# Offsets of a deformable convolution as a thread of their own in a four-layer network kernel

## The chip, the cores and the metric

The kernel runs on one core of a Trainium2 chip. The core has a matmul engine (TensorE, PE in the profile; PEld are its weight loads), VectorE (DVE), ScalarE (ACT), GpSimd (POOL) and SyncE (SP), which issues most of the transfers. Each engine works through its own instructions in program order, and waits between engines go over semaphores. The metric is the device time of one execution in microseconds (us). The times of the kernel before are 12860.76, 12851.66 and 12822.62 us, median 12851.66 us.

## The reference

The input is a batch of four images of 56x56 positions with 128 channels, in float32. Four residual layers follow each other; each takes the group norm of x (32 groups) and adds its result to x. Layers 0 and 3 are window attention, then attention over all 3136 positions with four heads, then an MLP of 128 to 512 to 128. Layer 1 is a selective scan in four directions after a depthwise 3x3 convolution. Layer 2, which the change is about, is a deformable 3x3 convolution:

```python
x = x + _L0_conv_ref(_gn(x), ...)
x = x + _L1_conv_ref(_gn(x), ...)
x = x + _L2_conv_ref(_gn(x), L2_conv_kernel, L2_conv_bias, L2_conv_offset_w, L2_conv_offset_b)
x = x + _L3_conv_ref(_gn(x), ...)
...
offsets = lax.conv_general_dilated(x, offset_w, ...) + offset_b
dy, dx = (offsets[..., 0], offsets[..., 1])
py = jnp.arange(H, ...)[None, :, None, None] + ky + dy
px = jnp.arange(W, ...)[None, None, :, None] + kx + dx
y0 = jnp.floor(py)
x0 = jnp.floor(px)
...
val = gather(y0i, x0i) * ((1 - wy) * (1 - wx))[..., None] + ...
out = jnp.einsum('bhwkc,kcf->bhwf', val, kernel.reshape(KK, C, F))
```

For each position and each of the nine taps a small convolution says how far from the regular place the sample is taken. Four neighbours are fetched, weighted and summed, and the nine samples are multiplied by the kernel.

## The kernel before

Channels lie on the 128 partitions and an image is a row of 3136 columns, cut into seven chunks of 448 (`NCK`, `CH`). Two images are held at a time (`x_of(b)` takes the buffer by the image's parity), so the layers of neighbouring images are staggered. `run` (L1476) sets the order. For image b it emits the attention of layer 0; then, woven together, the MLP of layer 0 and the convolution stage of layer 1 for image b (`first_half`, L1464) with layer 2 of image b-1 (`deform`, L1282); then the scan of layer 1 (`mamba`, L763); and then layer 3 of image b-1 (`last_layer`, L1471). Image 3 has no successor, so its layer 2 goes beside the MLP of layer 3 of image 2, and the last call is layer 3 of image 3 with nothing beside it.

`weave` (L650) takes two generators, a main and a side one. Each yields a number, a planned duration, and the one whose sum is lower is continued (the side one if equal). So the numbers set only the order in which the instructions of the two stand in each engine's queue.

`deform` has two parts. The first, L1310 to L1391, finds the offsets: it takes the group norm, writes the normed image x to a table in device memory with positions as rows (transposes at L1324, copies at L1325, eight DMAs on the SP queue at L1333), runs the offset convolution as 63 matmuls of 32 output rows in two groups (L1353), adds the bias (L1362), transposes (L1365), and then works out indices `idx` and weights `wts` in twelve VectorE steps per group (L1372 to L1390). Its yields sum up to 7 x 0.6 + 8 x 0.8 = 10.6. The second part, L1392 to L1456, has 84 units (chunk, row of three taps, block of 112 positions). A unit is three indirect DMAs on the POOL queue (`gather`, L1300), three VectorE operations (`weigh`, L1406 to L1408), six transposing matmuls and a ScalarE copy (`turn`, L1418 and L1419), and, four units later, a product with the kernel (L1426). `lead = 4` units are gathered ahead into six buffers; the first four are asked for in the middle of the first part (L1382), as soon as the first group's indices stand. A unit yields 1.9. The weights of both parts, 973 KB, are one pack "L2" that `deform` loads at its head.

`mlp` (L662) is a pipeline over the seven chunks. What matters here is that its PSUM banks depend on whether it is alone: `bufs={"mm": 6 if alone else 2, "pc": 2 if alone else 1}` (L667). All matmul results but the centred rows ("pc") go through the "mm" banks. `last_layer` passes `side is None` for `alone`. The yields of an MLP sum up to 69.8, those of the convolution stage of layer 1 (`mamba_conv`, L772) to 91.0.

Of the kernel before, what the change touches and what calls it, by code (L numbers as in the profile page):

```python
# [10 lines left out]
F32 = mybir.dt.float32  # L11
F32R = mybir.dt.float32r
I32 = mybir.dt.int32
# [6 lines left out]
P = 128  # L20
# [34 lines left out]
def _swin_cols():  # L55
# [7 lines left out]
    "L0": _swin_cols(),  # L63
    "L1": [("w_in", 512), ("w_xproj", 2 * NX), ("w_out", 256), ("conv_w", 18), ("conv_b", 2), ("b_dt", 2),
           ("A_log", 2 * NST), ("D", 2), ("ln_w", 2), ("ln_b", 2), ("w_dt", 256)],
    "L2": [("kernel", KK * 128), ("offset_w", KK * 32), ("bias", 1), ("offset_b", 1), ("base", 2 * KK * NTB)],
    "L3": _swin_cols(),
}

# [9 lines left out]
class _Net:  # L79
# [1199 lines left out]
                )  # L1279
                nc.sync.dma_start(t[TR * TR :], z[:1])  # L1280

    def deform(self, b):  # L1282

# [3 lines left out]
        tab = self.tables[b]  # L1287
        n2 = NTB * KK
        nq = CH // QB
        lead = 4  # L1290
        units = [(c, j, i) for c in range(NCK) for j in range(KK // 3) for i in range(nq)]
        with tc.tile_pool(name="df", bufs=1, side="right") as s1, tc.tile_pool(name="df_ps", bufs=1, space=PSUM, side="right") as s1x:
            self.load("L2", s1, nc.sync)
            w = self.w["L2"]
            idx = s1.tile([QB, n2], I32, tag="idx", name="idx")
            wts = s1.tile([QB, n2, 4], F32, tag="wts", name="wts")
            wps = s1x.tile([P, 3, nq * KK, 4], F32, tag="wt", name="wt")
            patch = {}

# [7 lines left out]
                        in_offset=bass.IndirectOffsetOnAxis(ap=idx[:, n : n + 1], axis=0),  # L1307
                    )

            with tc.tile_pool(name="dc", bufs=1, side="right") as sb, tc.tile_pool(name="dc_ps", bufs=4, space=PSUM, side="right") as ps:  # L1310
                bank = lambda name: ps.tile([P, 512], F32, tag="mm", name=name)
                gp = sb.tile([P, TR, TR], F32, tag="gp", name="gp")
                nc.gpsimd.memset(gp, 0.0)
                gn = self.group_norm(b, sb, bank)
                xg = sb.tile([P, L], F32, tag="xg", name="xgd")
                gt = sb.tile([QB, NTB, P], F32, tag="gt", name="gt")
                tv = tab[: TR * TR].rearrange("(t r x) (k c) -> r x t k c", r=2, x=TR, k=2)
                for c in range(NCK):
                    cols = slice(c * CH, (c + 1) * CH)
                    self.gn_apply(xg[:, cols], x[:, cols], gn)  # L1320
                    pt = bank("pgt")
                    for i in range(nq):
                        t = c * nq + i
                        nc.tensor.transpose(pt[:QB, i * P : (i + 1) * P], xg[:, t * QB : (t + 1) * QB], self.ident)  # L1324
                    nc.scalar.copy(gt[:, c * nq : (c + 1) * nq, :].rearrange("q t c -> q (t c)"), pt[:QB, :])  # L1325
                    if c in (3, NCK - 1):
                        ts = slice(0 if c == 3 else 4 * nq, (c + 1) * nq)
                        for k in range(2):
                            for r in range(2):

                                y = r + 1 - k
                                dst = tv[y % 2, 1 : 1 + HW, y // 2 + ts.start : y // 2 + ts.stop, k, :]
                                nc.sync.dma_start(dst, gt[r * HW : (r + 1) * HW, ts, :])  # L1333
                    yield 0.6
                gv = xg.rearrange("p (h w) -> p h w", w=HW)
                of = sb.tile([P, 2, CH], F32, tag="of", name="of")
                pos, fl, up = (sb.tile([QB, 2 * n2], F32, tag=n, name=n) for n in ("pos", "fl", "up"))
                fi = sb.tile([QB, 2 * n2], I32, tag="fi", name="fi")
                ix = sb.tile([QB, n2], F32, tag="ix", name="ix")
                fr = sb.tile([QB, 2, 2 * n2], F32, tag="fr", name="fr")  # L1340
                for g in range(2):
                    n = min(4, NCK - 4 * g)
                    rows = slice(32 * g, min(HW, 32 * g + 32))
                    nc.vector.tensor_copy(gp[:, 1 + rows.start : 1 + rows.stop, 1 : 1 + HW], gv[:, rows, :])
                base = w["base"][:QB, :]
                for g in range(2):
                    n = min(4, NCK - 4 * g)
                    pf = bank("pf")
                    for k in range(KK):
                        ky, kx = k // 3, k % 3  # L1350
                        for j in range(n):
                            c = 4 * g + j
                            nc.tensor.matmul(  # L1353
                                pf[32 * j : 32 * j + 32, :CH].rearrange("p (h w) -> p h w", w=HW),
                                lhsT=w["offset_w"][:, k * 32 : (k + 1) * 32],
                                rhs=gp[:, 8 * c + ky : 8 * c + ky + 8, kx : kx + HW],
                                start=(k == 0),
                                stop=(k == KK - 1),
                            )
                        if k % 3 == 2:  # L1360
                            yield 0.8
                    nc.scalar.activation(of[: 32 * n, g, :], pf[: 32 * n, :CH], AF.Identity, bias=w["offset_b"][: 32 * n, :])  # L1362
                    pt = bank("pof")
                    for i in range(nq):
                        nc.tensor.transpose(pt[:QB, i * P : i * P + 32 * n], of[: 32 * n, g, i * QB : (i + 1) * QB], self.ident[: 32 * n, : 32 * n])  # L1365
                    src = pt[:QB, :].rearrange("q (i j s) -> q j i s", j=4, s=32)[:, :n, :, : 2 * KK]

                    ts = slice(4 * g * nq, (4 * g + n) * nq)
                    ns = slice(ts.start * KK, ts.stop * KK)
                    both = lambda t: t[:, 2 * ns.start : 2 * ns.stop]  # L1370
                    view = lambda t: both(t).rearrange("q (j i s) -> q j i s", j=n, s=2 * KK)
                    nc.vector.tensor_add(view(pos), src, view(base))  # L1372

                    nc.vector.tensor_scalar(both(pos), both(pos), -1.0, float(HW), ALU.max, ALU.min)
                    nc.vector.tensor_copy(both(fi), both(pos))
                    nc.vector.tensor_copy(both(fl), both(fi))
                    nc.vector.tensor_tensor(both(up), both(fl), both(pos), ALU.is_gt)
                    nc.vector.tensor_sub(both(fl), both(fl), both(up))
                    fl2 = both(fl).rearrange("q (n s) -> q n s", s=2)
                    nc.vector.scalar_tensor_tensor(ix[:, ns], fl2[:, :, 0], float(TR), fl2[:, :, 1], ALU.mult, ALU.add)  # L1380
                    nc.vector.tensor_scalar_add(idx[:, ns], ix[:, ns], float(TR + 1))
                    if g == 0:  # L1382
                        for u in range(lead):
                            gather(u)
                    nc.vector.tensor_sub(both(fr[:, 1, :]), both(pos), both(fl))
                    nc.vector.tensor_scalar(both(fr[:, 0, :]), both(fr[:, 1, :]), -1.0, 1.0, ALU.mult, ALU.add)
                    for k in range(4):
                        wy = fr[:, k % 2, :].rearrange("q (n s) -> q n s", s=2)[:, :, 0]
                        wx = fr[:, k // 2, :].rearrange("q (n s) -> q n s", s=2)[:, :, 1]
                        nc.vector.tensor_mul(wts[:, ns, k], wy[:, ns], wx[:, ns])  # L1390
                    yield 0.8  # L1391
# [81 lines left out]
            x1, oT = self.swin_attention("L3", b, s1)  # L1473
            self.weave(self.mlp("L3", b, x1, oT, True, side is None), side)

    def run(self):  # L1476
        self.nc.sync.dma_start(self.xs[0], self.x_in[0])
        self.swin_prepare("L0")
        self.swin_prepare("L3")
        self.mamba_prepare()  # L1480
        self.deform_prepare()
        self.nc.sync.dma_start(self.xs[1], self.x_in[1])
        for b in range(self.B):
            for c in range(NCK):
                self.stats(b, c)
            with ExitStack() as mb:
                s1, made = ExitStack(), {}
                made["at"] = self.swin_attention("L0", b, s1)
                self.weave(self.first_half(b, s1, mb, made, b == 0), self.deform(b - 1) if b > 0 else None)
                self.mamba(b, made["pool"], made)  # L1490
            if b > 0:
                self.last_layer(b - 1, self.deform(b) if b == self.B - 1 else None)
        self.last_layer(self.B - 1)


# [53 lines left out]
def _packs(inputs):  # L1549
    def getter(layer):  # L1550
        return lambda n: np.ascontiguousarray(inputs[f"{layer}_conv_{n}"])

    parts = {"C": _constants(), "L0": _swin_pack(getter("L0")), "L1": _mamba_pack(getter("L1")),
             "L2": _deform_pack(getter("L2")), "L3": _swin_pack(getter("L3"))}
# [29 lines left out]
```

## Time and profile before

| what | us |
|---|---|
| median of the runs | 12851.66 |
| the profiled execution's own time | 12830.39 |
| its span | 12828.6 |
| layer 0 MLP and convolution of image 0, nothing beside them | 878 to 1073 |
| the same for image 1, beside layer 2 of image 0 | 2932 to 3399 |
| the same for image 2, beside layer 2 of image 1 | 6096 to 6562 |
| the same for image 3, beside layer 2 of image 2 | 9251 to 9720 |
| layer 3 MLP of images 0 and 1, nothing beside it | 5261 to 5329, 8419 to 8487 |
| layer 3 MLP of image 2, beside layer 2 of image 3 | 11579 to 12000 |

The stretches are cut where one kind of instruction ends and the next begins, so that each holds one stage. Over the span PE is busy for 11489.0 us (90%), DVE 9912.4 (77%), POOL 9659.9 (75%) and ACT 7461.7 (58%). The rest of the span is attention (PE busy all the time) and scan (DVE and POOL busy all the time), which the change does not touch. In a row of the view by stretches each engine has its busy time and, in brackets, its number of instructions. In a row of the view in order of time stand start, duration, engine, line, operation, output and inputs, shape and count, and in square brackets how long the engine had been idle and what ended that.

### The profile page before, as it was taken

What the parts mean: (1) busy time and instruction counts of PE and PEld (TensorE: products, weight loads), DVE (VectorE), ACT (ScalarE), POOL (GpSimd) and SP (SyncE); (2) the same over time, 40 slices, a digit from 0 to 9 for tenths busy, and PEclk for the clock granted to TensorE, in tenths of its full rate; (3) what the DMA queues carried; (4) which work ended last, traced back from release to release, by engine and by line L of the source; (5) the groups of instructions that cost most, each with busy time, mean ns of one, the idle gap of its engine ahead of it and who ended that gap; (6) DMA issues with size and microseconds to landing.
All of it is one profiled execution on the core that took longest, in us unless ns stands there. A gap on an engine that the chain in (4) does not pass through costs nothing.

```text
span 12828.6 us, 220823 instructions
## 1 busy us (share of the span) xinstructions
PE 11489.0 (90%) x86708; PEld 7481.4 (58%) x86708; DVE 9912.4 (77%) x12555; ACT 7461.7 (58%) x19090; POOL 9659.9 (75%) x6636
## 2 busy tenths in 40 slices
PE   5998998997799899999789989989978998996699
PEld 3546886543588755454368875545436886543454
DVE  4758997776999867576799977747589997776675
ACT  3567776553577655656367765565536776553356
POOL 1866996686799748578689975848778996686487
PEclk8999999998899999999889999999989999997899
DMA  1000000004200000000420000000051000004200
GB/s 62 1 1 17 5 5 2 1 1 123 86 5 5 3 1 1 11 1 1 144 66 5 5 2 1 1 11 1 19 155 38 5 5 1 1 1 138 62 1 6
DMA packets 155231, 321.13 MB, mean 25 GB/s; under 512 B 19612, under 2 KB 88400, under 8 KB 153936
## 3 DMA queue, kind: packets, MB, share of 16 engines
q0 software_dynamic: 80640, 231.28, 6.2%
q1 hardware_dynamic: 73264, 74.14, 1.9%
q8 instruction: 685, 11.22, 0.4%
q14 instruction: 354, 2.90, 0.1%
q10 hardware_dynamic: 288, 1.59, 0.0%
HBM read 259.03 MB, written 47.90 MB: 24 GB/s over the span
## 4 chain that ended last, share of the span: by engine, by line
PE 63%; DVE 20%; ACT 7%; issue 4%; POOL 4%; another core or an unknown queue 2%; SPq 1%; DMA 0%; DVEq 0%; ACTq 0%; POOLq 0%
PE pm L367 17%; DVE hs L1115 12%; PE po L573 10%; PE pst L546 5%; PE yt L1133 4%; PE dbu L1097 4%; PE pst L537 3%; POOL hs L1124 3%; PE pyb L1149 3%; PE pd L562 2%; DVE dgb L1001 2%; PE pss L276 1%; PE ph L703 1%; PE pt L1068 1%
## 5 line engine op out<-in xcount | busy, mean ns | idle before, releaser
L368 DVE TENSOR_REDUCE mx<-pm 128x1 f32<-128x256 f32 (+2 forms) x5600 | 3263.0, 618 | 1082.1 <-PE pm L367 1065.3
L557 POOL TENSOR_TENSOR es<-es,e 128x896 f32<-128x896 f32 x1824 | 3769.4, 2090 | 297.3 <-ACT e L547 249.5
L547 ACT ACTIVATE e<-pst 128x448 f32<-128x448 f32 (+1 forms) x5600 | 2591.8, 549 | 1857.9 <-PE pst L546 999.4
L1115 DVE TENSOR_TENSOR_SCAN hs<-da,dbu 128x928 f32<-128x928 f32 x1792 | 3631.8, 2069 | 50.2 <-ACT dbu L1108 27.6
L1124 POOL TENSOR_TENSOR hs<-hs,cb 128x896 f32<-128x896 f32 x1792 | 3460.3, 1941 | 22.4 <-ACT carry L1119 17.3
L367 PE MATMUL pm<-ks,qs 32*128 32x256 f32 (+2 forms) x11200 | 3133.0, 586 | 13.9 <-DVE nm L389 7.8
L546 PE MATMUL pst<-qs,ks 32*128 32x448 f32 x11200 | 2285.8, 536 | 0.0
L1133 PE MATMUL yt<-w_C,hs 128*116 128x128 f32 x14336 | 1863.6, 273 | 1.2 <-POOL hs L1124 1.2
L367 PEld LDWEIGHTS pm<-ks,qs 32*128 32x128 f32 x11200 | 1217.3, 186 | 975.3 <-DVE mx L368 598.1
L537 PE MATMUL pst<-nm,sel 32*128 32x448 f32 x5600 | 1659.9, 552 | 0.0
L1133 PEld LDWEIGHTS yt<-w_C,hs 128*116 128x116 f32 x14336 | 1569.1, 135 | 2.1 <-POOL hs L1124 2.1
L1097 PE MATMUL dbu<-dgb,ut 112*128 112x224 f32 x7168 | 1254.7, 297 | 271.3 <-DVE hs L1115 271.3
L546 PEld LDWEIGHTS pst<-qs,ks 32*128 32x128 f32 x11200 | 1369.8, 185 | 53.0
L1305 POOL DMA_INDIRECT g<-tab,idx x1008 | 1050.7, 1042 | 447.2 <-issue 264.7
L573 PE MATMUL po<-e,va 128*32 128x448 f32 (+1 forms) x11200 | 1350.9, 551 | 0.0
L1097 PEld LDWEIGHTS dbu<-dgb,ut 112*128 112x128 f32 x7168 | 942.0, 191 | 536.4 <-DVE hs L1115 526.6
L1051 ACT ACTIVATE da<-dl,A 128x112 f32<-128x112 f32 x3584 | 1193.9, 382 | 0.1
L294 POOL TENSOR_TENSOR pz<-s,m 64x784 f32<-64x784 f32 x128 | 191.8, 1499 | 847.6 <-DVE m L291 615.3
L537 PEld LDWEIGHTS pst<-nm,sel 32*128 32x128 f32 x5600 | 689.8, 184 | 180.2 <-issue 152.2
L573 PEld LDWEIGHTS po<-e,va 128*32 128x32 f32 (+1 forms) x11200 | 222.2, 107 | 966.7 <-issue 894.7
L1119 ACT COPY carry<-hs 128x32 f32<-128x32 f32 x1792 | 396.5, 221 | 624.0 <-DVE hs L1115 616.1
L557 POOL TENSOR_TENSOR es<-e 128x896 f32<-128x896 f32 x112 | 231.7, 2092 | 588.2 <-ACT e L547 588.2
(233 smaller groups left out, 15885.4 us busy)
## 6 DMA issues: line engine op xcount, KB each, us to landing
g<-tab,idx POOLq DMA_INDIRECT x1008
tab<-zero SPq DMA_DIRECT2D x4, 3364.0 KB
dl_d<-dl SPq DMA_DIRECT2D x28, 448.0 KB
dl<-dl_d SPq DMA_DIRECT2D x56, 224.0 KB
tab<-gt SPq DMA_DIRECT2D x16, 448.0 KB
out_dram<-x SPq DMA_DIRECT2D x28, 224.0 KB
tab<-gt SPq DMA_DIRECT2D x16, 336.0 KB
w_L<-in_L_dram SPq DMA_DIRECT2D x4, 973.0 KB
```

What stands on the lines that cost most here:

```text
L367: nc.tensor.matmul(pm[:, :m], lhsT=qs[head(h), q.start : q.start + P], rhs=ks[head(h), keys], start=True, stop=True)
L368: nc.vector.tensor_reduce(mx[:, home[i][1], h, kc : kc + 1], pm[:, :m], AX.X, ALU.max)
L537: nc.tensor.matmul(pst[g, h][:, :CH], lhsT=self.sel[head(h), :], rhs=nm[head(h), part(g // NKB)], start=True, stop=False)
L546: nc.tensor.matmul(t[:, :CH], lhsT=ks[head(h), k * KB : (k + 1) * KB], rhs=qs[head(h), part(qc)], start=False, stop=True)
L547: nc.scalar.activation(es[g, p][:nk, j, :], t[:nk, :CH], AF.Exp, scale=SCALE)
L557: nc.gpsimd.tensor_tensor(s, es[g - 1, p][:nk] if k == 1 else s, es[g, p][:nk], ALU.add)
L573: nc.tensor.matmul(m["po"][head(h), :CH], lhsT=va[:nk, k, head(h)], rhs=src(h)[:nk], start=(k == 0), stop=(k == NKB - 1))
L1051: nc.scalar.activation(m["da"][:, :, n, 2:], dl(), AF.Exp, scale=A[:, j, n : n + 1])
L1097: nc.tensor.matmul(pu[:, 8 * h : 8 * h + 8, 2 + tb * TB : 2 + (tb + 1) * TB], lhsT=made[g]["ut", 2 * r + tb][:, d, :], rhs=made["r", g // ...
L1115: nc.vector.tensor_tensor_scan(flat(pairs[u // 2][:, d % 2]), flat(made[g]["da"][:, r]), flat(banks.pop(u)), 0.0, ALU.mult, ALU.add)
L1124: nc.gpsimd.tensor_tensor(hs, hs, made["r", g // 2]["cb"][:, :, r * HW : (r + 1) * HW], ALU.mult)
L1133: nc.tensor.matmul(sums[q][:YR, e * P : (e + 1) * P], lhsT=hs[:, n, :], rhs=self.ident, start=(n == 0), stop=(n == NST // 2 - 1), is_trans ...
```

## The change

The first part of `deform` becomes a generator of its own, `offsets(b, where, pace)`, with all its yields multiplied by `pace`. Its results `idx` and `wts` live in a pool "dx" of their own, which stays open until the units of that image are done. The pack "L2" is split: "O2" with what the offsets need, and "L2" with kernel and bias. `deform` keeps the units alone; it asks for the first four gathers at its head. `run` places the offsets of image 0 after the scan of image 0, with nothing beside them; those of images 1 and 2 beside the MLP of layer 3 of the preceding image, with pace 4; those of image 3 directly before its `deform`, in one thread with it, as before.

```diff
-    "L2": [("kernel", KK * 128), ("offset_w", KK * 32), ("bias", 1), ("offset_b", 1), ("base", 2 * KK * NTB)],
+    "L2": [("kernel", KK * 128), ("bias", 1)],
+    "O2": [("offset_w", KK * 32), ("offset_b", 1), ("base", 2 * KK * NTB)],
...
+    def offsets(self, b, where, pace=1):
...
+        s1 = where.enter_context(tc.tile_pool(name="dx", bufs=1, side="right"))
+        idx = s1.tile([QB, n2], I32, tag="idx", name="idx")
+        wts = s1.tile([QB, n2, 4], F32, tag="wts", name="wts")
+        self.found = idx, wts
+        with tc.tile_pool(name="dc", bufs=1, side="right") as sb, tc.tile_pool(name="dc_ps", bufs=4, space=PSUM, side="right") as ps:
+            bank = lambda name: ps.tile([P, 512], F32, tag="mm", name=name)
+            self.load("O2", sb, nc.sync)
+            w = self.w["O2"]
...
+                yield 0.6 * pace
...
+                    if k % 3 == 2:
+                        yield 0.8 * pace
...
+                    nc.vector.tensor_mul(wts[:, ns, k], wy[:, ns], wx[:, ns])
+                yield 0.8 * pace
+
+    def deform(self, b):
...
+        idx, wts = self.found
         lead = 4
...
             self.load("L2", s1, nc.sync)
             w = self.w["L2"]
-            idx = s1.tile([QB, n2], I32, tag="idx", name="idx")
-            wts = s1.tile([QB, n2, 4], F32, tag="wts", name="wts")
...
-                    if g == 0:
-                        for u in range(lead):
-                            gather(u)
...
+            for u in range(lead):
+                gather(u)
...
+    def both(self, *threads):
+        for t in threads:
+            yield from t
...
                 self.weave(self.first_half(b, s1, mb, made, b == 0), self.deform(b - 1) if b > 0 else None)
+                if b > 0:
+                    where.close()
                 self.mamba(b, made["pool"], made)
-            if b > 0:
-                self.last_layer(b - 1, self.deform(b) if b == self.B - 1 else None)
+            where = ExitStack()
+            if b == 0:
+                self.weave(self.offsets(b, where))
+            elif b + 1 < self.B:
+                self.last_layer(b - 1, self.offsets(b, where, 4))
+            else:
+                self.last_layer(b - 1, self.both(self.offsets(b, where), self.deform(b)))
+                where.close()
         self.last_layer(self.B - 1)
```

More of the change, by code (lines that the diff above doesn't have):

```diff
@@ L1280, in deform_prepare @@
                 nc.sync.dma_start(t[TR * TR :], z[:1])
-    def deform(self, b):
+    def offsets(self, b, where, pace=1):
         nc, tc, x = self.nc, self.tc, self.x_of(b)
@@ L1289, in deform @@
         nq = CH // QB
+        s1 = where.enter_context(tc.tile_pool(name="dx", bufs=1, side="right"))
[6 more added lines that the diff above has]
+            w = self.w["O2"]
+            gp = sb.tile([P, TR, TR], F32, tag="gp", name="gp")
+            nc.gpsimd.memset(gp, 0.0)
+            gn = self.group_norm(b, sb, bank)
+            xg = sb.tile([P, L], F32, tag="xg", name="xgd")
+            gt = sb.tile([QB, NTB, P], F32, tag="gt", name="gt")
+            tv = tab[: TR * TR].rearrange("(t r x) (k c) -> r x t k c", r=2, x=TR, k=2)
+            for c in range(NCK):
+                cols = slice(c * CH, (c + 1) * CH)
+                self.gn_apply(xg[:, cols], x[:, cols], gn)
+                pt = bank("pgt")
+                for i in range(nq):
+                    t = c * nq + i
+                    nc.tensor.transpose(pt[:QB, i * P : (i + 1) * P], xg[:, t * QB : (t + 1) * QB], self.ident)
+                nc.scalar.copy(gt[:, c * nq : (c + 1) * nq, :].rearrange("q t c -> q (t c)"), pt[:QB, :])
+                if c in (3, NCK - 1):
+                    ts = slice(0 if c == 3 else 4 * nq, (c + 1) * nq)
+                    for k in range(2):
+                        for r in range(2):
+                            y = r + 1 - k
+                            dst = tv[y % 2, 1 : 1 + HW, y // 2 + ts.start : y // 2 + ts.stop, k, :]
+                            nc.sync.dma_start(dst, gt[r * HW : (r + 1) * HW, ts, :])
+                yield 0.6 * pace
+            gv = xg.rearrange("p (h w) -> p h w", w=HW)
+            of = sb.tile([P, 2, CH], F32, tag="of", name="of")
+            pos, fl, up = (sb.tile([QB, 2 * n2], F32, tag=n, name=n) for n in ("pos", "fl", "up"))
+            fi = sb.tile([QB, 2 * n2], I32, tag="fi", name="fi")
+            ix = sb.tile([QB, n2], F32, tag="ix", name="ix")
+            fr = sb.tile([QB, 2, 2 * n2], F32, tag="fr", name="fr")
+            for g in range(2):
+                n = min(4, NCK - 4 * g)
+                rows = slice(32 * g, min(HW, 32 * g + 32))
+                nc.vector.tensor_copy(gp[:, 1 + rows.start : 1 + rows.stop, 1 : 1 + HW], gv[:, rows, :])
+            base = w["base"][:QB, :]
+            for g in range(2):
+                n = min(4, NCK - 4 * g)
+                pf = bank("pf")
+                for k in range(KK):
+                    ky, kx = k // 3, k % 3
+                    for j in range(n):
+                        c = 4 * g + j
+                        nc.tensor.matmul(
+                            pf[32 * j : 32 * j + 32, :CH].rearrange("p (h w) -> p h w", w=HW),
+                            lhsT=w["offset_w"][:, k * 32 : (k + 1) * 32],
+                            rhs=gp[:, 8 * c + ky : 8 * c + ky + 8, kx : kx + HW],
+                            start=(k == 0),
+                            stop=(k == KK - 1),
+                        )
+                    if k % 3 == 2:
+                        yield 0.8 * pace
+                nc.scalar.activation(of[: 32 * n, g, :], pf[: 32 * n, :CH], AF.Identity, bias=w["offset_b"][: 32 * n, :])
+                pt = bank("pof")
+                for i in range(nq):
+                    nc.tensor.transpose(pt[:QB, i * P : i * P + 32 * n], of[: 32 * n, g, i * QB : (i + 1) * QB], self.ident[: 32 * n, : 32 * n])
+                src = pt[:QB, :].rearrange("q (i j s) -> q j i s", j=4, s=32)[:, :n, :, : 2 * KK]
+                ts = slice(4 * g * nq, (4 * g + n) * nq)
+                ns = slice(ts.start * KK, ts.stop * KK)
+                both = lambda t: t[:, 2 * ns.start : 2 * ns.stop]
+                view = lambda t: both(t).rearrange("q (j i s) -> q j i s", j=n, s=2 * KK)
+                nc.vector.tensor_add(view(pos), src, view(base))
+                nc.vector.tensor_scalar(both(pos), both(pos), -1.0, float(HW), ALU.max, ALU.min)
+                nc.vector.tensor_copy(both(fi), both(pos))
+                nc.vector.tensor_copy(both(fl), both(fi))
+                nc.vector.tensor_tensor(both(up), both(fl), both(pos), ALU.is_gt)
+                nc.vector.tensor_sub(both(fl), both(fl), both(up))
+                fl2 = both(fl).rearrange("q (n s) -> q n s", s=2)
+                nc.vector.scalar_tensor_tensor(ix[:, ns], fl2[:, :, 0], float(TR), fl2[:, :, 1], ALU.mult, ALU.add)
+                nc.vector.tensor_scalar_add(idx[:, ns], ix[:, ns], float(TR + 1))
+                nc.vector.tensor_sub(both(fr[:, 1, :]), both(pos), both(fl))
+                nc.vector.tensor_scalar(both(fr[:, 0, :]), both(fr[:, 1, :]), -1.0, 1.0, ALU.mult, ALU.add)
+                for k in range(4):
+                    wy = fr[:, k % 2, :].rearrange("q (n s) -> q n s", s=2)[:, :, 0]
+                    wx = fr[:, k // 2, :].rearrange("q (n s) -> q n s", s=2)[:, :, 1]
+                    nc.vector.tensor_mul(wts[:, ns, k], wy[:, ns], wx[:, ns])
+                yield 0.8 * pace
@@ L1290, in deform @@
+    def deform(self, b):
+        nc, tc, x = self.nc, self.tc, self.x_of(b)
+        tab = self.tables[b]
+        nq = CH // QB
+        idx, wts = self.found
         lead = 4
@@ L1308, in gather @@
                     )
[L1310 to L1381, printed above, removed]
-                    if g == 0:
-                        for u in range(lead):
-                            gather(u)
[L1385 to L1391, printed above, removed]
@@ L1553, in _packs @@
     parts = {"C": _constants(), "L0": _swin_pack(getter("L0")), "L1": _mamba_pack(getter("L1")),
-             "L2": _deform_pack(getter("L2")), "L3": _swin_pack(getter("L3"))}
+             "L2": _deform_pack(getter("L2")), "O2": _deform_pack(getter("L2")), "L3": _swin_pack(getter("L3"))}
     out = {}
```

## The prediction

> **What bounds it now.** I read the view by stretches first, because the change moves work between stages with different limits. Columns: stretch, its length, busy time (instructions) of PE, PEld, DVE, ACT and POOL, granted clock, DMA share, GB/s.
>
> ```profile
> 2932.00:3399.00 467.00, 339.06 (x1225) 174.94 (x1224) 379.43 (x480) 168.89 (x288) 291.30 (x276) 0.81 0.49 142
> 5261.00:5329.00 68.00, 62.04 (x166) 29.64 (x162) 40.10 (x40) 46.05 (x62) 17.73 (x18) 0.97 0.13 41
> 11579.00:12000.00 421.00, 242.08 (x966) 132.68 (x962) 293.32 (x346) 89.72 (x164) 251.00 (x267) 0.74 0.52 152
> ```
>
> In the first stretch (image 1's MLP and convolution with image 0's layer 2; two more are like it) DVE is the fullest engine, at 81%. The second, the MLP of layer 3 alone, is PE's, at 91%. The third is layer 2 of image 3 beside an MLP; its end is that of layer 2.
>
> The order of time at the head of the first stretch shows what the offsets cost there.
>
> ```profile
> 2939.49 0.35 DVE L134 BATCH_NORM_AGGREGATE gn_mv<-gn_st 128x2 f32<-128x42 f32 x1 [1.30 <-POOL oTi L599]
> ...
> 2943.70 0.51 DVE L150 TENSOR_SCALAR xgd<-x,gn_mean,gn_rstd 128x448 f32<-128x448 f32 x1
> ...
> 2959.31 5.83 PE L1353 MATMUL pf<-gp,w_L 128*32 128x448 f32 x48
> ...
> 2973.43 1.13 POOL L1305 DMA_INDIRECT g<-tab,idx  x1 [6.12 <-DVE idx L1381]
> ...
> 2985.83 0.96 DVE L1390 TENSOR_TENSOR wts<-fr 112x108 f32<-112x108 f32 x4
> 2986.63 1.02 DVE L1406 TENSOR_TENSOR pa<-g,wt 112x768 f32<-112x768 f32 x1
> ```
>
> Attention's last write frees the memory at 2939.5; the first unit is weighed at 2986.6, behind the last weights. For 47.1 us there are no units, though they set the stage's end: the last is weighed until 3376.2, the last statistics end at 3383.2, while the convolution's last DVE work ends at 3364.9.
>
> The same view in the MLP alone:
>
> ```profile
> 5283.79 2.95 DVE L688 RECIPROCAL ln_sq<-ln_sq 128x448 f32<-128x448 f32 x1 [1.83 <-ACT ln_sq L187]
> 5284.84 1.67 PE L703 MATMUL ph<-xn,w_L 128*128 128x448 f32 x4
> 5286.34 0.92 PE L160 MATMUL ln_pc<-x,w_C 128*128 128x448 f32 x2
> 5286.66 0.58 DVE L715 SCALAR_TENSOR_TENSOR x<-py,w_L,x 128x448 f32<-128x448 f32 x1
> 5287.16 0.61 DVE L692 TENSOR_TENSOR ln_sq<-ln_pc,ln_sq 128x448 f32<-128x448 f32 x1
> ...
> 5293.11 1.29 PE L703 MATMUL ph<-xn,w_L 128*128 128x448 f32 x3
> ```
>
> A chunk takes 8.27 us (5284.84 to 5293.11) with eleven matmuls of 0.75 us back to back: PE has no slack here, so what PE gets in addition lengthens the stage. Note too that the centred rows' matmul (L160) starts at 5286.34, before DVE has read the rows before them (L692, 5287.16), and that L715, which empties a bank, stands behind the reciprocal.
>
> **Step 1, units without the offsets before them (three stages).** `deform` can gather as soon as memory is free. Its first weighing follows two further gathers of 1.24 us and the landing; in image 3's units, where DVE waits for the DMA, 3.5 us pass from the start of a unit's third gather to the weighing (11934.47 to 11937.95). So 2939.5 + 0.3 + 2.5 + 3.5 = 2945.8 instead of 2986.6. What the MLP did in those 47 us must now be done beside units. Counting L1408, 32 units were done at the MLP's last store (3131.1; 4.5 us a unit) and 80 at the convolution's end (3363.8; 4.85 a unit). By the yields the MLP (69.8) now spans 69.8 / 1.9 = 36.7 units, and the convolution (91.0) the remaining 47.3: 36.7 x 4.5 + 47.3 x 4.85 = 394.5, so the last weighing ends at 3340.3, plus the same 7.0 us of tail, 3347.3 instead of 3383.2. **-35.9 a stage; I take -35, three times: -105.** Fifteen gathers now stand at the head of POOL's queue, before the MLP's addition (L683); only L715, many us later, needs that. The smaller load of "L2" on SP is wanted by the first product, some 20 us in; the load of 973 KB had landed within 20 us at 2959.3. Ends: -25 (a dense start: the first seven units took 5.4 us each) and -42 (the MLP costs nothing beside units; in image 3's tail without it a unit still takes 4.2).
>
> **Step 2, image 0's offsets with nothing beside them.** They come after the scan of image 0, and every engine's queue holds them ahead of the next attention. Added up from the rows above and those between: group norm 4.2 (2939.49 to 2943.70), seven applications 3.6, the first padded copy (L1344) 1.0, first group of matmuls 5.83 + 2.46 = 8.3, bias and transposes 1.4, second group 2.46 + 4.71 = 7.2, bias and transposes 1.4, twelve DVE steps 4.5: 31.6, and about 1.4 for the hand-overs. **+33** (30 to 40). The fill of `gp` (2.9 on POOL), the load of "O2" and the eight table DMAs (12.0 of SP's issuing) lie beside it; uncovered, the load could add some 5.
>
> **Step 3, images 1 and 2's offsets beside an MLP (two stages).** Both are PE work now.
> - Head: PE's queue begins with the group norm, which waits for the freed memory. The MLP's first matmul, at 5263.17 today, stands behind 5267.4 + 5.7 = 5273.1; its start-up had gaps, so I count +8.5.
> - Matmuls: transposes 3.5, offset convolution 15.5, two turns 1.2 and two waits of 0.75 for the bias on ACT: +21.5.
> - Banks: with "mm" at 2 the second hidden matmul waits until L715 has emptied the result's bank, which waits for the reciprocal (5286.74); with one "pc" bank L160 waits for L692 (5287.77). Followed through one chunk, the period comes to 10.15 instead of 8.27. Over seven chunks +13; offset matmuls lie in these holes in the first four chunks and the last two have no reciprocal, so +8.
> - DVE: gn, copies and 2 x 12 steps, 15 us on an engine busy 40 of 68. Mostly hidden, but a lump of 4.5 delays the reciprocal twice: +3. Some of the early transposes lie in start-up gaps: -3.
>
> Sum +38; **twice, +76**. Ends: +25 (only PE's 21.5 and part of the head) and +50 (with pace 1 beside image 3, the first hidden matmul came at 11618.9, 39.8 after the freed memory, against 7.4 in the MLP alone, so 32 there, and 13 for banks and some more at the end). The table DMAs stand on SP ahead of the stores and the loads of the next image; they are issued within the first quarter, and the last load is what the next stage waits for (8.5 us of DVE's idle time at L123, as before).
>
> Here the Trainium skill speaks against the change: "Perfetto Trace Analysis", sections "Matmuls" and "Matmul Optimizations", wants independent matmul groups to rotate through different PSUM banks and all eight used. Taken as a price, with nothing filling the holes, the rows give 13 a stage and the sum below rises by 10; I take 8, because here the side thread's matmuls fill most holes.
>
> **Step 4, image 3.** Its gathers were asked for inside the first part (11613.2 by the order of time); now they come behind the last weights, at 11633, because the unit's buffers lie where the offsets' were. First weighing at 11639.2 instead of 11632.6: **+7** (0 to 20; 20 if the gathers, not the weighing, set the pace of the stage. Units wait for landings only in the second half).
>
> **Sum:** -105 + 33 + 76 + 7 = **+11 us**. The profiled execution took 12830.4 (span 12828.6), so 12841 on its scale; it lies 21 us below the median shown, on whose scale I forecast 12851.7 + 11 = **12863**. A measurement of this kernel can tell about 0.3%, 38.6 us, from no change; the runs shown spread over 38. So the forecast is: no change that can be told.
>
> **Rivals.**
> - *The MLPs take the offsets badly (slower).* One place, layer 3 of images 0 and 1: two banks keep PE waiting in every chunk, and the offsets' chain, in order on PE, adds its whole length: 13 + 42 = +55 each. -105 + 33 + 110 + 7 = +45: 12897. For it: PE is full there, and the 32 us at image 3. Against it: pace 4 spreads the chain over 42.4 of 69.8. It decides from +52 a stage.
> - *The three stages are DVE's (slower).* Then only the DVE work taken out counts: about 16 us of 379 at 81%, 20 a stage. -60 + 33 + 76 + 7 = +56: 12908. For it: DVE is at 98% beside the convolution. Against it: beside the MLP it is near 80%, and in the first 40 us about half idle.
> - *Both ends good (faster).* The MLP is nearly free beside units (-42), and the layer-3 MLPs hide the chain in PE's own waits (+22): -126 + 33 + 44 + 7 = -42: 12810. For it: 4.5 us a unit with the MLP, 4.2 without. Against it: PE is full.
>
> That the move does not take place in time can be left out: nothing in queue order keeps the gathers behind the next attention's end.
>
> **How the numbers follow.** Forecast 0.45, first rival 0.20, second 0.17, faster 0.18. The ends together: 3 x -25 + 40 + 100 + 20 = +85 and 3 x -42 + 30 + 50 + 0 = -46; the range is 12800 to 12935. From the cases: faster 0.18, same 0.44, slower 0.38; the forecast's own spread crosses the upper bound a little.
>
> **What would show it.** First weighing about 6 us after attention's end in three stages, and these near 431 us instead of 467 (between 425 and 442 is right). A hole of about 33 us without scan or attention after image 0's scan. Layer 3's MLP of images 0 and 1 near 106 us, with PE waiting at L703 on L715 and at L160 on L692. Image 3's stage longer by 7. I am wrong if an MLP stage grows by over 50 or under 25, if units in the three stages take over 5 us each, or if something in attention slows, which now runs with the indices' 5 KB per partition kept.

## The result, and the profile after

The kernel with the change takes 12904.12 us (median of 6 runs, 12894.7 to 12916.09), the kernel before, on the same chip, 12852.24 us (6 runs, 12822.62 to 12867.71). The ratio is 1.0043, with a 95% interval of 1.003 to 1.0056: slower by 52 us, a little more than the 0.3% that can be told from no change. The profiled execution is the slowest of the six, 12916.09 us with a span of 12914.3, so the two traces differ by 85.7 us where the medians differ by 51.9. The stages show where.

The view by stretches of the kernel after has the same columns as before. The rows are image 1's MLP and convolution with image 0's layer 2; layer 3's MLP of image 0, now with the offsets of image 1; layer 2 of image 3; and image 0's offsets with nothing beside them, up to the end of the group norm of the attention behind them.

```profile
2998.60:3428.50 429.90, 306.21 (x1038) 162.66 (x1038) 358.83 (x431) 162.69 (x274) 282.00 (x274) 0.82 0.51 146
5294.80:5412.00 117.20, 92.43 (x320) 39.09 (x320) 50.98 (x76) 51.21 (x71) 19.72 (x18) 0.89 0.20 55
11663.70:12084.40 420.70, 240.88 (x950) 132.91 (x950) 287.44 (x335) 88.02 (x162) 246.34 (x262) 0.74 0.54 152
2197.20:2229.50 32.30, 21.54 (x170) 11.10 (x170) 16.26 (x49) 5.80 (x12) 2.78 (x4) 0.87 0.40 100
```

The first stage is shorter, as meant, and its DVE is fuller: 358.83 of 429.90 is 83%. The second row carries the loss. PE worked 92.43 of 117.20 us, 79%, where the MLP alone had it at 91%. So the stage has grown by more than the work put into it: PE waits there. Its granted clock is lower too, 0.89 where the MLP alone had 0.97. That is a mean of full and half clock. Here are two of the five stretches at half clock, two matmuls in the first of them, and two at full clock (each matmul leaves two records):

```profile
5310.00:5316.90 6.90, 5.58 (x10) 2.53 (x10) 2.08 (x4) 2.14 (x4) 1.13 (x1) 0.51 0.00 0
5320.30:5323.70 3.40, 3.15 (x8) 1.93 (x9) 1.57 (x4) 1.99 (x3) 0.00 (x0) 0.50 0.14 33
...
5311.81 1.70 PE L161 MATMUL ln_pc<-x,w_C 128*128 128x448 f32 x2
5313.31 1.70 PE L677 MATMUL py<-oTi,w_L 128*128 128x448 f32 x2
...
5325.26 1.67 PE L704 MATMUL ph<-xn,w_L 128*128 128x448 f32 x4
```

From one matmul's start to the next it is 1.50 us in the first stretch, where the MLP alone had 0.75, and the two matmuls that start in the second (5321.44, shown below) take 2.79 us instead of 1.67. The five stretches hold 25.6 us, 20.1 of them with PE busy; in the MLP alone there was one stretch of 3.4, all of it busy. As a matmul takes half as long at full clock, some 8 us of the 55 that the stage has grown by are slower matmuls (half of 20.1 - 3.4; an estimate).

The table measures every stage in the same way in both traces, from attention's last write on POOL (from the scan's end for image 0) to what follows the stage. The 3.3 us of image 0 before are the group norm of the attention behind it.

| part | forecast | before, us | after, us | difference |
|---|---|---|---|---|
| the three stages, up to the first scan | -105 | 459.4, 459.9, 462.3 | 429.9, 430.7, 430.7 | -90.3 |
| image 0's offsets alone, with the attention behind them | +33 | 3.3 + 764.8 | 32.3 + 769.1 | +33.3 |
| layer 3 MLP of images 0 and 1, up to the last store | +76 | 62.1, 62.1 | 117.2, 117.7 | +110.7 |
| layer 2 of image 3 | +7 | 411.0 | 420.7 | +9.7 |
| sum | +11 | | | +63.4 |

The remaining 22.3 us of the two spans' difference lie ahead of the change. From the start to the end of image 0's first attention the execution took 885.0 us before and 908.1 after; in the profiles of the experiments, which share that code, it took 877.8 to 888.9. I take it for variation of that one execution. The 63.4 us of the touched stages are of the size of the medians' 51.9.

The order of time of the kernel after shows both ends of the first of the three stages.

```profile
2997.49 1.13 POOL L600 TENSOR_TENSOR oTi<-ou,rest 128x448 f32<-128x448 f32 x1 [5.89 <-DVE rest L596]
2998.91 1.13 POOL L1398 DMA_INDIRECT g<-tab,idx  x1 [0.29 <-POOL oTi L600]
...
3005.40 0.96 DVE L1419 TENSOR_TENSOR pa<-g,wt 112x768 f32<-112x768 f32 x1 [8.06 <-DMA g<-tab,idx]
...
3395.41 0.95 DVE L1421 TENSOR_TENSOR g<-g,pa 112x768 f32<-112x768 f32 x1
...
3407.80 1.09 DVE L872 SCALAR_TENSOR_TENSOR dl<-dl,sp_u 128x896 f32<-128x896 f32 x1
...
3408.81 0.68 DVE L1443 SCALAR_TENSOR_TENSOR x<-pdo,w_L,x 128x448 f32<-128x448 f32 x1
...
3412.03 0.27 DVE L938 MEMSET carry<- 128x256 f32 x1 [1.88 <-DMA dl_d<-dl]
```

The first gather leaves POOL 0.3 us after attention's last write, and the first weighing comes 6.8 us after it instead of 47. The units end 397.7 us after it (436.7 before). But the last addition to x (L1443) now stands in DVE's queue right behind the convolution's last step (L872), 13.1 us after the last unit's work, where the tail was 6.3. And ahead of the scan DVE waits until the convolution's `dl` is written (L938). The units no longer set the end of the stage alone.

The same view at the head of the MLP of layer 3:

```profile
5294.83 0.34 DVE L135 BATCH_NORM_AGGREGATE gn_mv<-gn_st 128x2 f32<-128x42 f32 x1 [1.30 <-POOL oTi L600]
...
5299.60 1.10 PE L1311 MATMUL pgt<-w_C,xgd 128*112 128x128 f32 x4 [2.44 <-DVE xgd L151]
...
5307.58 2.95 DVE L689 RECIPROCAL ln_sq<-ln_sq 128x448 f32<-128x448 f32 x1 [0.73 <-ACT ln_sq L188]
5310.45 0.41 DVE L151 TENSOR_SCALAR xgd<-x,gn_mean,gn_rstd 128x448 f32<-128x448 f32 x1
...
5310.92 1.10 PE L1311 MATMUL pgt<-w_C,xgd 128*112 128x128 f32 x4 [4.04 <-DVE xgd L151]
...
5317.20 2.95 DVE L689 RECIPROCAL ln_sq<-ln_sq 128x448 f32<-128x448 f32 x1 [1.48 <-ACT ln_sq L188]
5320.07 0.41 DVE L151 TENSOR_SCALAR xgd<-x,gn_mean,gn_rstd 128x448 f32<-128x448 f32 x1
...
5320.55 1.10 PE L1311 MATMUL pgt<-w_C,xgd 128*112 128x128 f32 x4 [4.04 <-DVE xgd L151]
5321.44 2.79 PE L704 MATMUL ph<-xn,w_L 128*128 128x448 f32 x4
```

The offsets' application of the group norm (L151) takes 0.41 us, but it stands in DVE's queue behind a reciprocal of the MLP (L689) of 2.95 us. The transposes (L1311) need it, and they stand in PE's queue ahead of the MLP's matmuls. So PE waits 4.04 us for a step of 0.41, twice in these lines, and the first hidden matmul (L704) comes at 5321.4, 26.6 us after attention's last write; before it came after 7.4.

The view of waits of this stage (engine, tile and line that waits, what for; us in total, times, longest):

```profile
PE pgt L1311 <- DVE xgd L151: 14.4, 5, 4.0
...
PEld ln_pc L161 <- DVE ln_sq L693: 5.9, 2, 4.4
PEld ph L704 <- ACT h L705: 5.5, 6, 1.4
...
PE gn_pm L137 <- DVE gn_mv L135: 5.5, 1, 5.5
```

The first row is that queue order: 14.4 us in five pieces. The next two are banks: a new matmul's weight load waits until the bank's reader is done; the matmuls themselves wait there for 4.5 and 2.2 us. The last is the group norm at the head of PE's queue; all but 0.5 us of that wait lies ahead of the stage's start. Late in the stage, where the offsets are over and the clock is full, the banks stand alone in the order of time:

```profile
5386.74 0.92 PE L704 MATMUL ph<-xn,w_L 128*128 128x448 f32 x2
5388.38 1.02 PE L704 MATMUL ph<-xn,w_L 128*128 128x448 f32 x2 [0.72 <-ACT h L705]
...
5396.61 0.92 PE L704 MATMUL ph<-xn,w_L 128*128 128x448 f32 x2
```

From hidden to hidden matmul a chunk takes 9.87 us (5386.74 to 5396.61), against 8.27 before.

### The profile page after: what moved, and what is told of

The parts are those of the page before. It is cut to its first block, busy times and chain, and to the rows that moved or that the text cites. A ratio compares the mean times of both kernels' runs of the same rounds, so it can differ in the third digit from the quotient of the medians.

```text
span 12914.3 us, 220814 instructions
## 1 busy us (share of the span) xinstructions
PE 11499.1 (89%) x86708; PEld 7486.0 (58%) x86708; DVE 9914.2 (77%) x12555; ACT 7453.8 (58%) x19084; POOL 9647.2 (75%) x6636
```

## The experiments

My theory after the result was that the 55 us a stage are three things: the offsets' own PE work, the fewer banks, and waits of PE for DVE steps that stand behind reciprocals. The rivals were that PE work counts little and waits count for all of it, and that the whole chain of the offsets adds its length. None of the runs changes the clock by itself, so the part that it has is read from the traces. Where the time of a single execution is given, it stands beside one run or more of the kernel before, made together with it.

### More banks for the MLP

```diff
-bufs={"mm": 6 if alone else 2, ...}
+bufs={"mm": {True: 6, False: 2, 4: 4}[alone], "pc": 2 if alone else 1}
-tc.tile_pool(name="dc_ps", bufs=4, ...)
+tc.tile_pool(name="dc_ps", bufs=2 if pace > 1 else 4, ...)
-                self.last_layer(b - 1, self.offsets(b, where, 4))
+                self.last_layer(b - 1, self.offsets(b, where, 4), 4)
```

> The changed kernel, but the layer-3 MLPs of images 0 and 1 have four general PSUM banks and two for the centred rows (two and one in the change; the offsets get two instead of four). Measured from attention's last write to the end of the MLP's last store: 62.1 us before, 117.2 and 117.7 changed. If the banks are a main part (theory 1): the steady chunk goes from 9.9 back to 8.3 us and the stage to about 105. If PE mostly waits for the offsets' VectorE steps queued behind reciprocals (theory 2): 114 or more. First hidden matmul 26.6 us after attention's last write in either case.

The two stages took 105.3 and 105.4 us instead of 117.2 and 117.7; the first hidden matmul stayed where it was, 26.8 us in. Among PE's waits of this stage none for a bank's reader is left. One execution: 12885.75, beside 12849.12 before. So the banks cost 12 us a stage, and the head, untouched by them, is another matter.

### Fewer banks with nothing beside the MLP

In the kernel before, with the banks that an MLP has beside another thread:

```diff
-                self.last_layer(b - 1, self.deform(b) if b == self.B - 1 else None)
+                self.last_layer(b - 1, self.deform(b) if b == self.B - 1 else None, False)
```

> The kernel before, with the layer-3 MLPs of images 0 and 1 given two general banks and one for the centred rows though nothing runs beside them. From attention's last write to the last store, 62.1 us in the kernel before: theory 1, and the chunk followed by hand in the prediction (10.15 us instead of 8.27): 72 to 76. If the banks matter little: under 66.

The stages took 80.1 and 79.3 us, 17.6 more than 62.1 on the mean, and over the 72 to 76 that I had expected. In the middle of the MLP the order of time of this kernel reads:

```profile
5302.57 0.58 DVE L715 SCALAR_TENSOR_TENSOR x<-py,w_L,x 128x448 f32<-128x448 f32 x1
5303.21 1.02 PE L703 MATMUL ph<-xn,w_L 128*128 128x448 f32 x2 [0.55 <-DVE x L715]
...
5309.78 2.95 DVE L688 RECIPROCAL ln_sq<-ln_sq 128x448 f32<-128x448 f32 x1 [1.05 <-ACT ln_sq L187]
5312.65 0.58 DVE L715 SCALAR_TENSOR_TENSOR x<-py,w_L,x 128x448 f32<-128x448 f32 x1
5313.29 1.02 PE L703 MATMUL ph<-xn,w_L 128*128 128x448 f32 x2 [1.01 <-DVE x L715]
```

The period is 10.08 us (5303.21 to 5313.29), as followed by hand in the prediction (10.15), and the mechanism is the one named there: the hidden matmul waits for L715, and that stands behind the reciprocal. Seven chunks at +1.8 are 13; the other 4.6 lie mostly at the start, where the first hidden matmul came after 11.3 instead of 7.4, and which I had left out. (The half clock is in both: 13.7 us of it here, 3.4 in the kernel before.) One execution: 12899.99. The MLPs explain 35 of the 51 us over the 12849.12 beside it; in this kernel the three stages with layer 2 took 469, 470 and 466 instead of 459 to 462, with the same code. That is how far a stage can move from one kernel to another without an edit to it.

### The applications on POOL

With the group norm's applications and the padded copies of images 1 and 2 moved from DVE to POOL, no reciprocal stands ahead of them:

```diff
-                self.gn_apply(xg[:, cols], x[:, cols], gn)
+                (nc.gpsimd if pace > 1 else nc.vector).tensor_scalar(xg[:, cols], x[:, cols], gn[0], gn[1], ALU.subtract, ALU.mult)
...
-                nc.vector.tensor_copy(gp[:, ...], gv[:, rows, :])
+                    nc.gpsimd.tensor_scalar(to, x.rearrange(...)[:, rows, :], gn[0], gn[1], ALU.subtract, ALU.mult)
```

> The changed kernel, with the seven applications of the group norm and the two padded copies of the offsets of images 1 and 2 on GpSimd instead of VectorE (nothing else moved). In the changed kernel PE waits 14.4 us in five pieces for these applications, which stand behind reciprocals in VectorE's queue. Theory 2: the stage goes from 117 to 100 to 104 us, the first hidden matmul from 26.6 to about 18 us after attention's last write. Theory 1 alone: 114 or more.

A miss: 122.3 and 121.2 us, worse than the change, and 12919.61 in one execution. The groups of this kernel on POOL (busy us, mean ns of one, idle time before) say why:

```profile
L1307 POOL TENSOR_SCALAR xgd<-x,gn_mean,gn_rstd 128x448 f32<-128x448 f32 x14 | 26.0, 1866 | 2.7 <-DVE gn_rstd L147 2.7
L1333 POOL TENSOR_SCALAR gp<-x,gn_mean,gn_rstd 128x1792 f32<-128x1792 f32 (+1 forms) x4 | 22.6, 5646 | 0.0
```

An application takes 1.87 us on POOL instead of 0.41 to 0.51 on DVE. Seven of them and two copies are 24 us in one row on one engine at the head of the stage. The place in the queue was mended and the duration took its place, so this run doesn't test the theory.

### Both of these together

The edits of the first and the third experiment in one kernel.

> Both edits, more banks and the applications on GpSimd. If the two causes are separate and together make up what the forecast missed: the stage at 90 to 94 us, near 62 + 21.5 of matmuls + 8.5 of the later start, and the execution about 50 us under the changed kernel. If it stays over 105, something third costs, and the matmuls of the offsets themselves are dearer than 21.5.

101.9 and 101.8 us, against 105.3 with the banks alone and over the 90 to 94 expected; 12883.47 in one execution. With the banks there, POOL was worth 3.5 us, without them it cost 4; why the sign turns was not looked into.

### A finer cut of the offsets

The banks of the first experiment; the offsets begin only when the MLP has started, the group norm comes in pieces with MLP steps between them, the seven applications become one, and bias, transposes and index steps are yielded apart:

```diff
+                yield 5.0
+                nc.vector.bn_aggr(mv, ...)
+                yield 1.0
...
+                self.gn_apply(xg, x, gn)
+                yield 2.0
...
-                self.gn_apply(xg[:, cols], x[:, cols], gn)
```

> The changed kernel with the banks of e1_banks, and the offsets of images 1 and 2 cut finer: the MLP's first five units of work go ahead, the group norm is emitted in three pieces with MLP work between, the seven applications are one VectorE operation, and bias, transposes and index steps stand apart. PE's and VectorE's work stays the same. If what is left of the stage's growth after e1_banks (62 to 105 us) is half waiting of PE in queue order behind the offsets' chain at the head (theory 2): the first hidden matmul 10 to 14 us after attention's last write instead of 26.8, the stage at 86 to 92 us. If it is the offsets' own PE work (theory 3): the first hidden matmul comes earlier, but the stage stays at 100 or more.

Both stages took 91.8 us. By stretches, in order of time and by waits, in this kernel:

```profile
5260.20:5352.00 91.80, 81.26 (x315) 36.35 (x313) 48.26 (x68) 50.64 (x71) 19.38 (x18) 0.94 0.25 70
```

```profile
5265.96 0.28 DVE L1307 BATCH_NORM_AGGREGATE gn_mv<-gn_st 128x2 f32<-128x42 f32 x1
...
5268.17 2.69 PE L704 MATMUL ph<-xn,w_L 128*128 128x448 f32 x4
...
5271.26 1.91 DVE L151 TENSOR_SCALAR xgd<-x,gn_mean,gn_rstd 128x3136 f32<-128x3136 f32 x1
5273.23 1.10 PE L1333 MATMUL pgt<-w_C,xgd 128*112 128x128 f32 x4 [2.37 <-DVE xgd L151]
```

```profile
PE pof L1378 <- ACT of L1373: 2.8, 2, 1.6
PE gn_pm L1310 <- DVE gn_mv L1307: 2.6, 1, 2.6
PE pgt L1333 <- DVE xgd L151: 2.4, 1, 2.4
```

PE is back at 89% of its stage, the hidden matmul comes 8.0 us in, and the wait for the applications is 2.4 us, against 15.0 with the banks alone. From 105.3 to 91.8, the finer cut brought 13.5 us a stage. Order in the queues is its main part, by that wait, but not all of it. The seven applications in one and the other steps take 3.4 us less of DVE (48.26 for 51.66). And the clock is 0.94 instead of 0.89: PE was busy for 7.9 us at half clock, against 16.5 with the banks alone, which by the estimate above is some 4 of the 13.5. The edit holds several cuts, and which of them brings how much wasn't tried apart. What remains over 62.1 is 29.7 us. One execution: 12840.47, beside 12839.75 (median of 11): even mended so, the change gains nothing that can be told.

### The finer cut with few banks

> e5_split with the change's narrow banks (two general ones and one for the centred rows, four for the offsets). In the changed kernel's order the banks cost 12 us a stage (117.4 to 105.3); in an MLP with nothing beside it 17.6 (62.1 to 79.7). If banks and order are separate costs: 91.8 + 12 = about 104 us. If the finer cut also fills the holes that the banks leave: 94 to 98. If it makes them worse: 107 or more.

The same cut on the banks of the change took 100.1 us in both stages (12893.84 in one execution, beside 12867.75, median of 16). Here the banks cost 8.3 us (100.1 against 91.8), in the coarse cut 12. So neither 104 nor the best case, and the prices of banks and order don't simply add up; that some of the holes of the banks are filled when the side thread has a matmul ready would fit, but wasn't followed. The 8 of the prediction is the price in this cut, not in that of the change.

### Fewer taps

The offset convolution with three of its nine taps; the matmuls of the other six are left out, for every image:

```diff
-                for k in range(KK):
+                for k in range(3):
...
-                            stop=(k == KK - 1),
+                            stop=(k == 2),
```

> The changed kernel with three of the nine taps of the offset convolution for every image; the other six are left out of the computation, and with them 42 of 63 small matmuls an image, 10.3 us of PE. If PE sets the layer-3 MLP stages (theory 3), each of them shortens by about 10 us, from 117 to 107, and the piece with image 0's offsets alone by 10 too. If waits for other engines set them (theories 1 and 2), the two stages shorten by less than 5, since PE then only waits longer, while image 0's still shortens by 10.

The 10.3 us of matmuls left out (two thirds of 15.5) shortened the MLP stages by 9.9 and 8.1 us, to 107.3 and 109.6; image 0's offsets alone and the attention behind them gained 7.8, of the 10 expected. One execution: 12863.17. PE work counts nearly one to one in these stages, in spite of PE's waits: it doesn't fall into the holes.

### The order changed in place

The rival way to the same end: the kernel before, with the offsets where they were, but with the yields of that part set to 0, so that they go ahead of the MLP in every queue:

```diff
-                    yield 0.6
+                    yield 0.0
...
-                            yield 0.8
+                            yield 0.0
...
-                    yield 0.8
+                    yield 0.0
```

> The kernel before with the yields of the offsets' part at zero, so that it stands in every queue ahead of the MLP it is woven with; nothing else changes. If the units' later start is what the offsets cost in these four stages, at 0.7 us of stage for 1 us of start (30 us for 41 in the changed kernel): first weighing 33 to 36 us after attention's last write instead of 47, each of the four stages 8 to 10 us shorter, together -30 to -40 us against the kernel before. If those stages are set by the sum of VectorE's work (the prediction's second rival): no change, within 10 us together.

12800.67 us (median of 8) against 12839.75 before, ratio 0.9975, interval 0.9964 to 0.9986. The three stages took 453.4, 450.1 and 455.7 us and that of image 3 406.2, together 27 less than in the trace of before: 6.0, 9.8, 6.6 and 4.8, mostly less than the 8 to 10 each that I had expected. The two traces differ by 31, nearly all the rest ahead of the edit; the medians of the runs above by 39, and their ratio gives 32. So 27 us are placed. The order of time at the head of the first stage:

```profile
2934.81 1.13 POOL L599 TENSOR_TENSOR oTi<-ou,rest 128x448 f32<-128x448 f32 x1 [5.87 <-DVE rest L595]
...
2961.60 1.13 POOL L1305 DMA_INDIRECT g<-tab,idx  x1 [22.70 <-DMA tab<-gt]
...
2965.67 0.92 DVE L1390 TENSOR_TENSOR wts<-fr 112x108 f32<-112x108 f32 x4
...
2967.73 0.96 DVE L1406 TENSOR_TENSOR pa<-g,wt 112x768 f32<-112x768 f32 x1 [1.14 <-DMA g<-tab,idx]
```

The first weighing comes 31.8 us after attention's last write instead of 47. What ends the wait now is the writing of the table: the gather waits for it until 2961.6, 3.6 us after the first group's weights began (2958.0). This is the fastest of all kernels of this study, and it needs none of the change's moves.

### The mixed version

The finer cut for images 1 and 2, and the offsets of images 0 and 3 with pace 0 directly ahead of their own units:

```diff
-                self.weave(..., self.deform(b - 1) if b > 0 else None)
+                self.weave(..., None if b == 0 else self.both(self.offsets(0, where, 0), self.deform(0)) if b == 1 else self.deform(b - 1))
...
-                self.weave(self.offsets(b, where))
+                pass
...
-                self.last_layer(b - 1, self.both(self.offsets(b, where), self.deform(b)))
+                self.last_layer(b - 1, self.both(self.offsets(b, where, 0), self.deform(b)))
```

> The finer cut of e5_split for images 1 and 2, and for images 0 and 3 the offsets directly ahead of their own units in one thread, ahead of the MLP in every queue as in e7_first. If the stages simply add up: image 0 takes back the 33 us of its lone place and loses the 34 it gained by it but for some 6 to 9, image 3 ends some 5 earlier than before, images 1 and 2 give 30 to 34 and cost 29.7: together -10 to -25 us against the kernel before, so less than e7_first's 39. If hiding the offsets beside the layer-3 MLP is worth more than the stages show, it is the fastest kernel: under 12800.

12846.63 us (median of 13) against 12867.75 before (16), ratio 0.998, interval 0.9972 to 0.9989: 21 us faster, within the 10 to 25 expected. But the stages don't bear that out. The three took 468.6, 437.4 and 428.1 us, the MLPs 92.0 and 90.0, image 3's stage 414.8. Against the trace of before, images 1 and 2 gain 57 and their MLPs cost 58, and the first stage and that of image 3 are 9 and 4 longer, where I had expected both to be shorter. So this trace is 14 us longer than that of before, which was taken at another time than the 16 runs; of those no trace was kept. Where the 21 us come from is open, and that the number was met is luck.

In the first stage the offsets stand ahead of the MLP as in the run before this one, and yet it took 15 us more. Its first gather stands behind the last weights instead of the first group's indices:

```profile
2971.64 1.14 POOL L1426 DMA_INDIRECT g<-tab,idx  x1 [29.00 <-issue]
...
2978.03 0.96 DVE L1447 TENSOR_TENSOR pa<-g,wt 112x768 f32<-112x768 f32 x1 [7.45 <-issue]
```

The first weighing comes 38.4 us after attention's last write (2939.7), 6.6 later than in that run, and still 9 earlier than in the kernel before. The stage is longer than both. So the start of the units alone doesn't set these stages; the rest wasn't followed.

## Why the prediction was off by 41 us

The time lies in the range, 41 us over the forecast of 12863 and 7 over the first rival's 12897; slower by 0.43%, it falls just beyond the bound that the forecast stayed within. Step 3 failed, by 35 us (110.7 for 76).

- **Step 1, the three stages.** Right in mechanism, a seventh too large: -90 for -105. The head is as worked out (first weighing +6.8, 6.4 and 6.6 us for +6.3), and the units were even quicker than the yields gave: the end of the last weighing moved by -39.0, -40.2 and -41.1 for -35.9. The term that was off is the tail, "plus the same 7.0 us": up to the last addition it is 13.1 for 4.6 to 6.3, because the convolution moved up by only 15 to 17 us and its last DVE steps stand ahead of that addition, and from there to the scan it is 2.5 longer. Over all kernels of the study these stages took 427 to 437 us in the change's order (the mixed version's first stage, of another order, is left out) and 459 to 470 in that of before, so the gain is some 30 (29 to 32 by the means of the kernels against 460.5 before).
- **Step 2, image 0.** +33.3 for +33, in part by luck. The chain itself added 29.0 us, 4 less than its rows were added up to. The other 4.3 came in the attention behind it, of which the prediction had nothing; its first 35.3 us ran at a granted clock of 0.78 instead of 0.88.
- **Step 3, head and DVE.** This is the failed step. "So I count +8.5" for the head: the first hidden matmul came 19 us later (26.6 for 7.4). "DVE: mostly hidden, +3": PE waited 14.4 us for applications. A row that warned of the head was misread: beside image 3 the first hidden matmul (11618.9) came 33.4 us after attention's last write (11585.5), not 39.8, so 26 later than in the MLP alone, close to the 19 that came here. I had asked what the small DVE steps do to the reciprocals, and not what the reciprocals do to the small steps, behind which PE's own queue was standing. The finer cut takes 13.5 us out of the stage, most of it by order. The clock is the term put at nothing: the rows of the prediction show it, 0.97 for the MLP alone, but the sum has nothing for a change of it, and some 8 us (the estimate above) are matmuls slowed by the half clock. Two of those stretches begin inside the waits of 4.04 us, so the waits may be what lowers the clock; no run shows that.
- **Step 3, banks.** +8 taken, 12 measured in the change, 8.3 in the finer cut, 17.6 with nothing beside. The price worked out from one chunk, 13 unfilled, lacked the start of the MLP (some 4). The rule of the Trainium skill ("Perfetto Trace Analysis", sections "Matmuls" and "Matmul Optimizations"), weighed at 13, was the better guide here: 12 were measured in the change. With nothing beside the MLP the banks cost 17.6, so the side thread does fill holes, but fewer than I took, except in the finer cut (8.3).
- **Step 3, matmuls.** The 21.5 us of PE work hold: three of nine taps took out 9.9 and 8.1 of 10.3 us. With the finer cut and the banks a stage still costs 29.7, and PE is idle for 10.5 of its 91.8 us (81.26 busy), against 3.8 of 62.1 in the MLP alone.
- **Step 4, image 3.** +9.7 for +7. The first weighing came 7.5 us later, for 6.6 worked out. Over the kernels of the study this stage took 420.7 to 433.3 in the change's order and 411.0 and 418.4 in that of before, so no more than the sign and the rough size is sure.
- **The rivals.** The first gave +55 a stage and the total of 12897, and that is what came, past its mark of 52 and past the 50 at which the prediction called itself wrong. But its account, 13 for banks and the chain's whole 42, isn't what the runs show: 12 banks, 13.5 the finer cut and about 30 for work and the waits that remain, with the slower clock in all three. The second, three stages bound by DVE with a gain of 20 each, falls: they gained 30, and the change of order in place, which takes no DVE work out, gained 6 to 10 there too. The third fell with the MLP stages: the chain doesn't hide in PE's waits.

Open: which cut inside the finer version brings its 13.5 us, what lowers the clock, why the mixed version's first stage is so long, and why stages of the same code differ by up to 10 us between kernels.

## What to carry to other kernels

Work put beside a stage whose engine is full cost more than its time on that engine here (21.5 us of matmuls became 28 to 30 at best, 55 as first written), and it must save more than that where it is taken away (some 30 here). Before moving a chain to another stage, try the order in place: letting the part that holds the others go first in every queue was worth 27 us by the stages and 39 by the medians, with three numbers changed. When two threads share in-order engines, look for a short step behind a long one of the other thread, and ask which engine's queue stands behind it: a step of 0.41 us behind a reciprocal of 2.95 held PE for 4.04. And read the clock of a stage before and after: a stage that waits more can also work more slowly.

## What the runs showed of the hardware

- The same TENSOR_SCALAR of 128x448 in float32 took 1.87 us on POOL and 0.41 to 0.51 on DVE; with 128x1792 it took 5.65 on POOL.
- One DVE application over 3136 columns took 1.91 us, against 3.05 for seven of 448 columns in a row (the run with the order changed in place): joining them saves about 1.1 us of DVE, and six places in a queue.
- The reciprocal of 448 columns took 2.95 us on DVE, where the other steps of that size shown here took 0.41 to 0.68.
- At a granted clock of 0.50 the matmuls of 128x448 followed each other after 1.50 us, and two of them took 2.79 us; at full clock it was 0.75, and 1.67 for two. The mean clock of the MLP stage was 0.97 alone, 0.89 in the change and 0.94 in the finer cut.
